# Fused conditioned attention on one core: the opening's load queues, one transposed chunk and three score bursts' banks are rearranged

## The chip, the core and the metric

The kernel runs on one core of a Trainium2 chip. The core has five engines that run side by side and meet through semaphores: TensorE (PE) multiplies matrices into PSUM, VectorE (DVE), ScalarE (ACT) and GpSimd (POOL) work elementwise, and SyncE (SP) issues transfers. PSUM has eight banks of 128 x 512 f32. Transfers can be issued from SP's queue or from ACT's; an engine takes its instructions in the order in which they stand, so whatever waits at the head of a queue holds up all that is behind it.

The metric is the device time of one execution in microseconds (us). The three timed runs of the kernel before took 762.27, 764.2 and 765.88 us; the median, 764.2 us, is its time.

## The reference

x has 8 batches of 512 rows and 512 columns (f32). There are 16 heads of 32 columns. `tokens` is the condition, one row for each batch.

```python
Q = _split_heads(x @ Wq.T + bq)
K = _split_heads(x @ Wk.T + bk)
V = _split_heads(x @ Wv.T + bv)
tQ = _split_heads(tokens @ Wq.T + bq)
tK = _split_heads(tokens @ Wk.T + bk)
cQ = Q + tQ
cK = K + tK
scores = einsum('bhqd,bhkd->bhqk', cQ, cK) / sqrt(HEAD_DIM)
attn = softmax(scores, axis=-1)
out = einsum('bhqk,bhkd->bhqd', attn, V)
return x + out
```

## The kernel before

The work is cut into 32 steps `t` (8 batches by 4 groups `g` of 128 columns, four heads in each). For a step, four chunks `qc` of 128 query rows are treated one after the other: a **burst** of four score matmuls (`row_scores`, L433, one head each, each shown as two passes in the profile, so x8) fills four banks, DVE takes the row maxima of two banks at a time (`row_max_of`, L442), and ACT makes the exponentials of these banks only to add up the denominators (`denominators`, L470, tile `dead`). Later the scores are made again transposed, with the maxima subtracted by a small matmul (L512, L515), ACT makes the exponentials `e` (L527, L529), and PE multiplies them with v (L534). The maxima reach the matmul as bf16 parts that POOL makes (`split_max`, L484 to L487) and PE transposes (`transpose_max`, L496). Projections are made in part by a fast scheme with seven products of half blocks (`first_products`, `other_products`, products at L335 and L338), which need sums of blocks of the weights (`combine_w`, POOL) and of x (`combine_x`).

The order of all work on PE, ACT, DVE and POOL is the order in which it is written (a manual schedule); the order of transfers is that of each issuing queue. A load needs a semaphore; there are eight for them in turn, so a later load waits, on its queue, for the landing of the load that holds its semaphore.

Everything before the loop `for t in range(T - 3)` is the **opening**. It loads four chunks of x (x0 to x3) and 12 chunks of weights (256 KB each), transposes them on PE (`transpose_x` L251, evacuated at L254; `transpose_w` L206, evacuated at L213 to L219), projects q and k of step 0 directly (L281), brings in the condition, and then runs the four bursts of step 0 and the first of step 1 between further projections.

Which bank is used where is written out by hand: `psum` is one tile of eight banks, `TURNS` holds one row for each burst, `banks(i)` is the i-th number in the current row, and `advance()` goes to the next. The places 4 to 7 of a row are the burst's four banks, in two pairs. The opening's bursts use rows 13 to 17:

```python
(2, 5, 0, 1, 6, 7, 3, 4),     # row 13: row_max(0, 0)
(2, 5, 3, 4, 6, 7, 0, 1),     # row 14: row_max(0, 1)
(0, 1, 5, 2, 6, 7, 3, 4),     # row 15: row_max(0, 2)
(0, 1, 5, 2, 6, 7, 3, 4),     # row 16: row_max(0, 3)
(5, 0, 6, 7, 1, 2, 3, 4),     # row 17: row_max(1, 0)
```

So the burst of `row_max(1, 0)` writes banks 1, 2, 3, 4, right after the burst of `row_max(0, 3)` in 6, 7, 3, 4. With `other_products("v", 0, 0, ..., (2, 0))` the products of v go to banks 6 and 5, and the maxima are transposed into bank 7.

The loads of the opening stand in this order. SP: x0, x2, the condition, bq, bk, Wq chunk 0, Wq 2 and 3, Wk 1 to 3, Wv 0 to 3, bv, then x4 to x7. ACT: x1, x3, Wk 0, Wq 1, and behind them the load of its table of functions with a first exponential (L193).

Of the kernel before, what the change touches and what calls it, by code (L numbers as in the profile page):

```python
# [17 lines left out]
def kernel(  # L18
# [33 lines left out]
    nc = tc.nc  # L52
    P = 128
    B, S, D = x.shape
# [5 lines left out]
    NS = S // P  # L60
# [33 lines left out]
        (2, 5, 0, 1, 6, 7, 3, 4),  # L94
        (2, 5, 3, 4, 6, 7, 0, 1),
        (0, 1, 5, 2, 6, 7, 3, 4),
        (0, 1, 5, 2, 6, 7, 3, 4),
        (5, 0, 6, 7, 1, 2, 3, 4),
    ]
    turn = [0]  # L100
# [1 line left out]
    def banks(i, n=1):  # L102

        j = TURNS[turn[0]][i]
        return psum[:, j, :] if n == 1 else psum[:, j : j + n, :]
# [13 lines left out]
    def load_x(n, queue=nc.sync):  # L119

        if n < B * NS:
            xs[n] = xp.tile([P, D], F32, tag="x", name=f"x_{n}")
            queue.dma_start(xs[n], x[n // NS, n % NS * P : (n % NS + 1) * P, :])
# [17 lines left out]
    def load_w(n, w, queue, cs=range(NC)):  # L141
        wv = w.rearrange("(c p) d -> p c d", p=P)
        for c in cs:
            queue.dma_start(ws[n][:, c, :], wv[:, c, :])
# [16 lines left out]
    load_x(3, nc.scalar)  # L161

    cond_sb = const.tile([B + 2, D], F32, tag="cond", name="cond_sb")
    nc.sync.dma_start(cond_sb[:B, :], cond)
    nc.sync.dma_start(cond_sb[B : B + 1, :], bq.rearrange("(o d) -> o d", o=1))
    nc.sync.dma_start(cond_sb[B + 1 : B + 2, :], bk.rearrange("(o d) -> o d", o=1))
    load_w("q", Wq, nc.sync, [0])
    load_w("k", Wk, nc.scalar, [0])
    load_w("q", Wq, nc.scalar, [1])
    load_w("q", Wq, nc.sync, [2, 3])  # L170
    load_w("k", Wk, nc.sync, [1, 2, 3])
    load_w("v", Wv, nc.sync)
    bvb = const.tile([P, D], F32, tag="bvb", name="bvb")
# [28 lines left out]
    def transpose_w(n, dc, pt, odd=None):  # L202

        odd = dc % 2 if odd is None else odd
        for cc in range(NC):
            nc.tensor.transpose(  # L206
                pt[:, cc * P : (cc + 1) * P], ws[n][:, dc, cc * P : (cc + 1) * P], ident
            )
        o = wT[n][:, :, dc * P : (dc + 1) * P]
        pv = pt.rearrange("p (c s) -> p c s", c=NC)  # L210
        if n == "q":
            if odd:
                nc.vector.tensor_scalar(o, pv, SCALE, None, ALU.mult)  # L213
            else:
                nc.scalar.activation(o, pv, AF.Copy, scale=SCALE)
        elif odd:
            nc.vector.tensor_copy(o, pv)
        else:
            nc.scalar.copy(o, pv)  # L219
# [3 lines left out]
    def combine_w(n):  # L223


        wc[n] = stage.tile([P, 4, 2, HS], F32, tag="w", name=f"wc_{n}")
        if n == "v":
            blk = wT[n].rearrange("p k (two f) -> p k two f", two=2)
            blk = [[blk[:, j * 2 : j * 2 + 2, i, :] for j in range(2)] for i in range(2)]
            to = [wc[n][:, i, :, :] for i in range(4)]  # L230
        else:
            blk = wT[n].rearrange("p k (u two f) -> p k u two f", u=2, two=2)
            blk = [[blk[:, j * 2 : j * 2 + 2, :, i, :] for j in range(2)] for i in range(2)]
            to = [wc[n][:, i, :, :].rearrange("p k (u f) -> p k u f", u=2) for i in range(4)]
        nc.gpsimd.tensor_tensor(to[0], blk[1][0], blk[1][1], ALU.add)
        nc.gpsimd.tensor_tensor(to[1], to[0], blk[0][0], ALU.subtract)
        nc.gpsimd.tensor_tensor(to[2], blk[0][0], blk[1][0], ALU.subtract)
        nc.gpsimd.tensor_tensor(to[3], blk[0][1], to[1], ALU.subtract)
# [4 lines left out]
    def transpose_x(n, pt, leaves=nc.vector.tensor_copy):  # L243

        b, sc = divmod(n, NS)
        if b >= B:
            return
        if sc == 0:
            xT[b] = xtp.tile([P, NC, S], F32, tag="xT", name=f"xT_{b}")
        for cc in range(NC):  # L250
            nc.tensor.transpose(  # L251
                pt[:, cc * P : (cc + 1) * P], xs[n][:, cc * P : (cc + 1) * P], ident
            )
        leaves(xT[b][:, :, sc * P : (sc + 1) * P], pt.rearrange("p (c s) -> p c s", c=NC))  # L254
        load_x(n + NS)
# [17 lines left out]
    def pair_of(t, n):  # L273

        if (n, t // 2) not in pairs:
            pairs[n, t // 2] = qkp.tile([P, 2, S], F32, tag=n, name=f"{n}T_{t // 2}")
        return pairs[n, t // 2]
# [50 lines left out]
    def product(n, b, u, i, pt, kcs=(0, 1), cols=None):  # L328


        for kc in kcs:
            w = block_of_w(n, i, u, kc)
            if n == "v":
                xb = block_of_x(b, i, kc, slice(u * P, (u + 1) * P))
                nc.tensor.matmul(pt, xb, w, start=(kc == kcs[0]), stop=(kc == kcs[-1]))  # L335
            else:
                xb = block_of_x(b, i, kc, cols or slice(0, HS))
                nc.tensor.matmul(pt, w, xb, start=(kc == kcs[0]), stop=(kc == kcs[-1]))  # L338

    def twice(a):  # L340
        return a.unsqueeze(1).broadcast_to([P, 2, HS])

    def halves(a):
        return a.rearrange("p (h s) -> p h s", h=2)


    def parts_of(n, b, u):

        if n == "v":
            v = vs[b % 2]  # L350
            return v[:, u::2, :HS], v[:, u + 2, :HS], v[:, u::2, HS:], v[:, u + 2, HS:]
        o = pair_of(b * G + u * 2, n)
        return halves(o[:, 0, :]), o[:, 0, HS:], halves(o[:, 1, :]), o[:, 1, HS:]

    def plus(n, b, u, g, o, pt, rest):

        if n == "v":
            nc.vector.tensor_tensor(o, pt, rest, ALU.add)
        else:
            add = tok[:, "qk".index(n), u * 2 + g, b : b + 1]  # L360
            nc.vector.scalar_tensor_tensor(o, pt, add, rest, ALU.add, ALU.add)
# [22 lines left out]
    def other_products(n, b, u, dens, small, at):  # L384

        dens()
        one_, two_ = banks(at[0]), banks(at[1])
        product(n, b, u, 4, one_[:, :HS])
        product(n, b, u, 5, one_[:, HS:])
        small()  # L390
        if n == "k":
            product(n, b, u, 2, two_[:, :P], (1,), slice(0, P))
            product(n, b, u, 2, two_[:, P:HS], (1, 0), slice(P, HS))
        else:
            product(n, b, u, 2, two_[:, :HS], (1,))
        product(n, b, u, 3, two_[:, HS:])
        c1, c12, c2, c22 = parts_of(n, b, u)
        nc.vector.tensor_tensor(c12, one_[:, HS:], c12, ALU.add)
        nc.vector.tensor_tensor(c2, halves(one_), twice(c22), ALU.add)
        plus(n, b, u, 0, c1, halves(two_), c1)  # L400
        if n != "v":
            for g in range(2):
                qkT[n, b * G + u * 2 + g] = pair_of(b * G + u * 2, n)[:, g, :]
# [60 lines left out]
    def denominators(t, qc, prs=range(NP)):  # L464

        if t >= T - 1:
            return
        for j in [pr * 2 + i for pr in prs for i in range(2)]:
            dead = op.tile([P, S], F32, tag="dead", name=f"dead_{t}_{qc}_{j}")
            nc.scalar.activation(  # L470
                dead,
                banks(HG + j),
                AF.Exp,
                bias=nmax[t][:, qc, j, :],
                accum_out=sums[t][:, qc, j, :],
            )
# [14 lines left out]
    def transpose_max(t, bank, copy=nc.vector.tensor_copy):  # L491
        if t >= T:
            return
        pt = bank.bitcast(BF16)
        for qc in range(NS):
            nc.tensor.transpose(  # L496
                pt[:, qc * P : (qc + 1) * P],
                split[t % 2][:, qc, :, :].rearrange("p h e -> p (h e)"),
                identb,
            )  # L500
        maxT[t] = op.tile([P, S], BF16, tag="maxT", name=f"maxT_{t}")
        copy(maxT[t], pt[:, :S])
# [125 lines left out]
    def bank(i):  # L628
        return psum[:, i, :]
# [37 lines left out]
    project_qk_end(0, "k", pk)  # L667
    transpose_w("v", 3, bank(4), 1)
    transpose_x(NS, bank(2), nc.scalar.copy)
    for n in ("q", "k", "v"):  # L670
        combine_w(n)

# [3 lines left out]

    turn[0] = 13
    row_max(0, 0)
    transpose_x(NS + 1, banks(0), nc.scalar.copy)
    denominators(0, 0)  # L680
    project_qk(1, "q", banks(3))
    project_qk(1, "k", banks(1))
# [11 lines left out]
    first_products("v", 0, 0, lambda: denominators(0, 3), nothing, 2, 0)  # L694
    advance()
    row_max(1, 0)
    transpose_max(0, banks(3), nc.scalar.copy)
    other_products("v", 0, 0, lambda: denominators(1, 0), nothing, (2, 0))
    load_residual(0)
    turn[0] = 0  # L700

# [25 lines left out]
    for t in range(T - 3):  # L727
# [53 lines left out]
        def small():  # L781
            transpose_max(t + 1, banks(1))
            if t and r % 2 == 0:
                output(t - 1, banks(2))
# [145 lines left out]
```

## Time and profile before

| What | Value |
|---|---|
| median of three runs | 764.2 us |
| the profiled execution itself | 762.58 us |
| its span, first to last instruction | 760.8 us |
| granted TensorE clock, mean over the span | 0.999 |
| DMA, mean over the span | 39 GB/s |
| DMA in the opening, 5 to 20 us | 311 to 371 GB/s |
| opening, start to first loop instruction on PE | 55.45 us |

The page of the profile gives each engine's busy time, the chain of waits that ended last, and groups of equal instructions. A timeline row gives start, duration, engine, line, operation, output<-inputs, shapes and count; where the engine was idle before it, the idle time and what ended it stand in square brackets. `PE` rows are matmuls, `PEld` rows the weight loads that go with them, `SPq` and `ACTq` rows the issue of a transfer. PE's ends are modelled: where two groups follow each other without a bracket, the difference of their starts is the time that the first one held PE. A chain row for a transfer gives the time of issue and the time until it landed.

The edited places lie at 0.7 to 10 us (loads, table, first transposes), 24 to 27 us (x4, x5 and the first burst) and 45 to 57 us (the last burst of step 0, the first of step 1, the transposed maxima and the products of v).

### The profile page before, as it was taken

Reading aid. Unit: us, or ns where it says so; the run is one execution under the profiler, and the core shown is the slowest. Engines: PE = TensorE matmul, PEld = TensorE weight load, DVE = VectorE, ACT = ScalarE, POOL = GpSimd, SP = SyncE. Lnnn points to the kernel's source line nnn. Section 1 sums busy time; section 2 is a strip of 40 time slices with the busy share of each in tenths; the row PEclk is TensorE's granted clock in tenths of the full one; section 3 lists DMA queues with packets and bytes.
Section 4 is the critical chain, followed back from the end, with each engine's and each line's share of the span. In section 5 each row is a group of like instructions: output and inputs, shape, how many; then the busy total and the mean of one; then the engine's idle time right before and its main releaser. Section 6 shows DMA issues by size and latency. Waiting matters only on the chain.

```text
span 760.8 us, 14393 instructions
## 1 busy us (share of the span) xinstructions
PE 750.4 (99%) x5494; PEld 435.9 (57%) x5494; DVE 525.2 (69%) x730; ACT 630.2 (83%) x1462; POOL 132.9 (17%) x229
## 2 busy tenths in 40 slices
PE   8999999999999999999999999999999999999997
PEld 5566556655556665565665555665555665555432
DVE  2577767677667777676776776777766777757764
ACT  2559888888889888888888888888888988888965
POOL 2711011111101111101111111111110111110220
PEclk9999999999999999999999999999999999999999
DMA  9200011102011110111111011110101111000110
GB/s 310 64 2 15 15 43 43 43 15 56 15 42 43 43 31 13 47 39 43 42 32 40 15 43 42 43 44 14 43 1 28 29 28 28 1 29 29 29 42 28
DMA packets 40376, 29.51 MB, mean 39 GB/s; under 512 B 1770, under 2 KB 34538, under 8 KB 40308
## 3 DMA queue, kind: packets, MB, share of 16 engines
q1 hardware_dynamic: 39460, 27.42, 12.6%
q10 hardware_dynamic: 848, 1.18, 0.5%
q8 instruction: 43, 0.70, 0.4%
q14 instruction: 25, 0.20, 0.1%
HBM read 20.21 MB, written 8.39 MB: 38 GB/s over the span
## 4 chain that ended last, share of the span: by engine, by line
PE 96%; ACT 1%; DMA 1%; DVE 0%; issue 0%; DVEq 0%
PE psum L338 25%; PE psum L534 15%; PE psum L515 15%; PE psum L433 14%; PE psum L335 14%; PE psum L512 6%; PE psum L566 2%; PE psum L251 2%; PE psum L281 2%; PE psum L496 1%; ACT e L527 1%; DMA w_k<-in_L_cond_Wk_dram 1%; PE psum L206 1%; ACT e L529 0%; DMA x<-in_x_dram 0%
## 5 line engine op out<-in xcount | busy, mean ns | idle before, releaser
L442 DVE TENSOR_REDUCE nmax<-psum 128x2 f32<-128x1024 f32 x256 | 301.7, 1219 | 160.1 <-PE psum L433 159.4
L470 ACT ACTIVATE dead<-psum,nmax 128x512 f32<-128x512 f32 x496 | 335.0, 692 | 12.9 <-DVE nmax L442 12.8
L527 ACT ACTIVATE e<-psum 128x512 f32<-128x512 f32 x270 | 145.8, 595 | 81.5 <-PE psum L515 81.5
L433 PE MATMUL psum<-kT,qT 32*128 32x512 f32 x1024 | 138.1, 595 | 0.7 <-ACT kT L296 0.4
L515 PE MATMUL psum<-qT,kT 32*128 32x512 f32 x1024 | 132.5, 588 | 0.0
L529 ACT ACTIVATE e<-psum 128x1024 f32<-128x1024 f32 x121 | 124.7, 1030 | 0.0
L534 PE MATMUL psum<-e,v 128*32 128x512 f32 x1024 | 118.6, 596 | 0.4 <-ACT e L529 0.3
L470 ACT ACTIVATION_READ_ACCUMULATOR dead<-psum,nmax 128x1 f32 x496 | 103.6, 209 | 0.0
L484 POOL CAST split<-nmax 128x16 bf16<-128x16 f32 x32 | 8.2, 255 | 510.8 <-DVE nmax L442 510.8
L433 PEld LDWEIGHTS psum<-kT,qT 32*128 32x128 f32 x1024 | 63.8, 183 | 51.8 <-issue 29.4
L534 PEld LDWEIGHTS psum<-e,v 128*32 128x32 f32 x1024 | 29.5, 109 | 82.1 <-issue 57.9
L512 PE MATMUL psum<-maxT,onesb 3*128 3x512 bf16 x512 | 51.4, 384 | 1.6 <-DVE res L580 0.8
L515 PEld LDWEIGHTS psum<-qT,kT 32*128 32x128 f32 x1024 | 51.1, 185 | 2.5 <-issue 0.2
L591 POOL TENSOR_TENSOR res<-res,xr 128x512 f32<-128x512 f32 x30 | 38.1, 1271 | 66.1 <-DVE res L580 66.1
L335 PE MATMUL psum<-wc_v,xc 128*128 128x256 f32 x192 | 49.4, 380 | 0.0
L512 PEld LDWEIGHTS <-onesb 3*128 3x128 bf16 x512 | 13.4, 91 | 60.5 <-issue 50.9
L338 PE MATMUL psum<-xc,wc_q 128*128 128x256 f32 x180 | 46.4, 380 | 0.3 <-ACT e L529 0.3
L338 PE MATMUL psum<-xc,wc_k 128*128 128x256 f32 x180 | 46.3, 379 | 0.0
L556 DVE COPY oT<-psum 128x512 f32<-128x512 f32 x29 | 20.1, 691 | 35.6 <-PE psum L534 35.6
L135 POOL TENSOR_TENSOR xr<-xr,bvb 128x512 f32<-128x512 f32 x32 | 40.6, 1270 | 0.0
L335 PE MATMUL psum<-wT_v,xT 128*128 128x256 f32 x128 | 37.9, 398 | 0.0
L335 PEld LDWEIGHTS psum<-wc_v,xc 128*128 128x128 f32 x192 | 35.4, 190 | 4.3
(147 smaller groups left out, 831.0 us busy)
## 6 DMA issues: line engine op xcount, KB each, us to landing
xr<-in_x_dram SPq DMA_DIRECT2D x32, 256.0 KB, 3.1
out_dram<-res SPq DMA_DIRECT2D x31, 256.0 KB, 2.4
x<-in_x_dram SPq DMA_DIRECT2D x30, 256.0 KB, 2.7
w_v<-in_L_cond_Wv_dram SPq DMA_DIRECT2D x4, 256.0 KB, 5.5
w_q<-in_L_cond_Wq_dram SPq DMA_DIRECT2D x3, 256.0 KB, 4.4
w_k<-in_L_cond_Wk_dram SPq DMA_DIRECT2D x3, 256.0 KB
x<-in_x_dram ACTq DMA_DIRECT2D x2, 256.0 KB, 4.1
w_k<-in_L_cond_Wk_dram ACTq DMA_DIRECT2D x1, 256.0 KB, 4.5
```

The costliest lines, as they stand in the source:

```text
L135: nc.gpsimd.tensor_tensor(xr[t], xr[t], bias, ALU.add)
L335: nc.tensor.matmul(pt, xb, w, start=(kc == kcs[0]), stop=(kc == kcs[-1]))
L338: nc.tensor.matmul(pt, w, xb, start=(kc == kcs[0]), stop=(kc == kcs[-1]))
L433: nc.tensor.matmul(pt, qkT["q", t][r, qc * P : (qc + 1) * P], qkT["k", t][r, :], start=True, stop=True,)
L442: nc.vector.tensor_reduce(nmax[t][:, qc, pr * 2 : pr * 2 + 2, 0], pt, AX.X, ALU.max, negate=True)
L470: nc.scalar.activation(dead, banks(HG + j), AF.Exp, bias=nmax[t][:, qc, j, :], accum_out=sums[t][:, qc, j, :],)
L512: nc.tensor.matmul(bank[j], onesb[r, :], maxT[t][r, :], start=True, stop=False)
L515: nc.tensor.matmul(bank[j], qkT["k", t][r, kc * P : (kc + 1) * P], qkT["q", t][r, :], start=False, stop=True,)
L527: nc.scalar.activation(e[:, i, :], bank[pr * 2 + i], AF.Exp)
L529: nc.scalar.activation(e, banks(2, 2), AF.Exp)
L534: nc.tensor.matmul(pt[j * HD : (j + 1) * HD, :], vs[b % 2][:, kc, (g * HG + j) * HD : (g * HG + j + 1) * HD], es[t, kc, j // 2][:, j % 2, ...
L591: last.tensor_tensor(y, y, xr.pop(t), ALU.add)
```

## The change

- The three small loads into `cond_sb` (the condition, bq, bk) are issued by ACT instead of SP, behind x1 and x3. Wk 0 and Wq 1 are issued by SP instead of ACT, behind Wq 0. ACT's table load then stands behind x1, x3 and the three small loads.
- The transposes of x5 with their copy on ACT stand ahead of the first burst instead of behind it, and go to bank 5 instead of bank 2.
- Row 16 of `TURNS` has its two pairs in the other order, so that `row_max(0, 3)` fills banks 3, 4, 6, 7. The transposed maxima of step 0 go to bank 0 instead of 7, and the second half of the v products uses banks 5 and 6 in the other order.

```diff
-        (0, 1, 5, 2, 6, 7, 3, 4),
+        (0, 1, 5, 2, 3, 4, 6, 7),
...
-    nc.sync.dma_start(cond_sb[:B, :], cond)
-    nc.sync.dma_start(cond_sb[B : B + 1, :], bq.rearrange("(o d) -> o d", o=1))
-    nc.sync.dma_start(cond_sb[B + 1 : B + 2, :], bk.rearrange("(o d) -> o d", o=1))
+    nc.scalar.dma_start(cond_sb[:B, :], cond)
+    nc.scalar.dma_start(cond_sb[B : B + 1, :], bq.rearrange("(o d) -> o d", o=1))
+    nc.scalar.dma_start(cond_sb[B + 1 : B + 2, :], bk.rearrange("(o d) -> o d", o=1))
     load_w("q", Wq, nc.sync, [0])
-    load_w("k", Wk, nc.scalar, [0])
-    load_w("q", Wq, nc.scalar, [1])
-    load_w("q", Wq, nc.sync, [2, 3])
+    load_w("k", Wk, nc.sync, [0])
+    load_w("q", Wq, nc.sync, [1, 2, 3])
...
     transpose_x(NS, bank(2), nc.scalar.copy)
+    transpose_x(NS + 1, bank(5), nc.scalar.copy)
...
     row_max(0, 0)
-    transpose_x(NS + 1, banks(0), nc.scalar.copy)
     denominators(0, 0)
...
-    transpose_max(0, banks(3), nc.scalar.copy)
-    other_products("v", 0, 0, lambda: denominators(1, 0), nothing, (2, 0))
+    transpose_max(0, banks(1), nc.scalar.copy)
+    other_products("v", 0, 0, lambda: denominators(1, 0), nothing, (0, 2))
```

## The prediction

> **What bounds the kernel now.** I read the page's first line and busy row, then the chain of waits, then the timeline and the chain in order of time for the first 60 us, because every edit lies before the main loop.
>
> ```profile
> span 760.8 us, 14393 instructions
> PE 750.4 (99%) x5494; PEld 435.9 (57%) x5494; DVE 525.2 (69%) x730; ACT 630.2 (83%) x1462; POOL 132.9 (17%) x229
> PE 96%; ACT 1%; DMA 1%; DVE 0%; issue 0%; DVEq 0%
> ```
>
> TensorE (PE) sets the end: 99% busy, 96% of the chain. So only what moves PE counts, and the change can win only the time in which PE stands still or crawls in the opening. The timeline of PE from 0 to 57 us has three such places besides its start.
>
> ```profile
> 8.89 0.63 PE L206 MATMUL psum<-ident,w_k 128*128 128x128 f32 x4 [1.16 <-DMA w_k<-in_L_cond_Wk_dram]
> 25.32 1.14 PE L433 MATMUL psum<-kT,qT 32*128 32x512 f32 x8 [0.39 <-ACT kT L296]
> 26.39 0.66 PE L251 MATMUL psum<-ident,x 128*128 128x128 f32 x4
> 49.93 2.18 PE L433 MATMUL psum<-kT,qT 32*128 32x512 f32 x8
> 52.04 0.40 PE L496 MATMUL psum<-identb,split 128*128 128x128 bf16 x4
> ```
>
> Columns: start, duration, engine, line, what, count, and in brackets the idle time before it and who ended it. See three things: 1.16 us of waiting for the first chunk of Wk; 0.39 us for kT; and a burst of eight score matmuls that takes 2.18 us where the same burst takes 1.14 everywhere else. The burst is slow without an idle bracket because half of it is held back; the weight loads show by whom:
>
> ```profile
> 50.99 0.29 PEld L433 LDWEIGHTS psum<-kT,qT 32*128 32x128 f32 x2 [0.38 <-ACT dead L470]
> ```
>
> **Part 1, the queues.** Before, ScalarE (ACT) issues two chunks of x, waits until chunk 0 of x has landed, issues Wk chunk 0, waits for chunk 2, issues Wq chunk 1, and only then loads its table:
>
> ```profile
> 4.22 0.34 ACTq L144 DMA_DIRECT2D w_k<-in_L_cond_Wk_dram  x1
> 5.52 0.34 ACTq L144 DMA_DIRECT2D w_q<-in_L_cond_Wq_dram  x1
> 5.88 1.28 ACT L193 ACT_TABLE_LOAD   x1 [5.88 <-DMA x<-in_x_dram]
> 7.29 1.05 ACT L254 COPY xT<-psum 128x512 f32<-128x512 f32 x2
> ```
>
> Wk0, issued at 4.22, lands 4.54 us later, at 8.76 (chain in order of time). Afterwards the three small loads (16 KB, 2 KB, 2 KB; 0.37, 0.23, 0.25 us of issue) leave SP and come behind x on ACT, and SP issues Wq0 at about 1.66, Wk0 at about 2.1, then Wq1 to Wq3. The built program has waits on SP at Wq1 (x0 landed, 4.20), Wq2 (x2, 5.50) and Wq3 (x3, 5.69), none at Wk0. The four x chunks still go first and share the same engines, so x stays at 4.20 to 5.69 and its transposes still end near 6.74. The weights then follow in the order of need: before, the chunks on SP alone land 0.67 us apart (12.58, 13.25, 13.93, 14.61 in the landing records). From Wq0 near 6.2 (6.34 before) this puts Wk0 near 6.9 and Wq1 near 7.6.
>
> PE then runs without the gap: bias and cond transposes 6.74, Wq0 7.08 (both as before), Wk0 at 7.53, Wq1 at 7.98 (a transposed chunk every 0.45 to 0.47, as from 9.56 to 10.03). The q projection needs wT_q0, which VectorE (DVE) has at 8.46 as before, so it starts at 8.49 instead of 10.03: **1.54 us won**. It also needs ACT's two copies of xT. ACT's last small load, bk, waits for x1 (4.38), so the table loads at about 4.7, not at 2.6; its first copy starts at 6.1, the second waits for PE's transposes (6.80) and ends at 7.42. That is 1.07 us of cover for the table's move. GpSimd's (POOL's) combinations of x start 0.9 earlier and bind nobody.
>
> A rule of the Trainium skill speaks against this part: "DMA: Bandwidth & Descriptors", section "Issuing engines are not separate DMA queues", says loads issued from different engines share the same 16 DMA engines, so that a change of issuer saves only the issue time. By it Wk0 would land as late as before and the part would be worth nothing on PE. The row says that Wk0 was late because its issue stood at 4.22 behind a wait and its packets then mixed with Wq2's, issued at 4.40; issue time and place in line do change. I take the row: 1.54 and not 0.
>
> The unknown is bk, now issued at about 4.40. PE's cond transposes wait for it, and every matmul is queued behind them; it costs nothing if landed by 6.61. Nearest row: Wk0, on ACT's queue at 4.22, had its first of 16 shares landed at 6.80, 2.58 later, of which some 0.6 are the seven further packets of 85 ns in a share; that leaves 1.98, so 6.38. Upper end by the undiminished 2.58: 6.98, which costs 0.37. Worst row: Wk0's full 4.54, so 8.94, a cost of 2.33. I take 6.38 and zero; less is impossible, since the x transposes end at 6.74 anyway.
>
> **Part 2, the chunk of x.** PE's 0.39 gap at 25.32 is the wait for kT, which ACT ends at 25.27. Four transposes now stand in it: they issue from 24.77 to 25.21, before kT is there, so the burst stays at 25.32 and the projection follows at 26.39 instead of 26.89: **0.50 us won**. Bank 5, their target, was emptied by DVE's qT (22.08 + 0.75 = 22.83) and is next written by the k projection, 3.4 us after the q projection starts; ACT's copy (0.59, behind x4's, so done by 26.35) is long over. On ACT it lies ahead of the exponentials, which wait for the maxima until 27.79: hidden. Its reload of x moves up on SP, from 27.08 to about 25.4 behind the 24.96 one; their order stays. If ACT were late with kT the gain would drop to 0.39.
>
> **Part 3, the banks.** Today's burst at 49.93 has its last two heads in banks 3 and 4, which the third and fourth exponential of the group before (49.48 and 50.15, read-out ended 50.27 and 50.94) still occupy. With that group's pairs swapped, 3 and 4 hold the first and second (read-out ended 48.93 and 49.60), free before 49.93. So the burst takes 1.07 from start to next start, as at 25.32, instead of 2.11: **1.04 us won**. What is late next, all on before's clock: the transposes of the maxima, now at 51.00, need POOL's split (semaphore 50.47) and the reader of bank 0 (DVE, 50.47): 0.5 to spare. Bank 6 is free at 50.27, bank 7 at 50.95; needed past 52 and at 54.4. ACT copies maxT 1.04 earlier, so the next four exponentials start with their maxima (52.33, 53.47) and release bank 4 near 55.1; DVE's last step on v ends near 55.3. The burst now at 56.54 wants both at 55.50: 0.2 to spare, the same as today (56.35 against 56.54). If one misses, the cost is the miss, up to the whole 1.04.
>
> **Sum:** 1.54 + 0.50 + 1.04 = 3.08 us, all of it time in which PE stands. From 55 us on PE has no gap over 0.03 us until 623 us, and nothing in the opening sits at a fixed time after the first loads, so the shift reaches the end. The profiled execution took 762.58 us (span 760.8): 759.5 (span 757.7). It lies 1.6 under the median of the runs, 764.2; from that median, **761.1**.
>
> **Rivals.** (a) One term fails, bk by 0.37 or more, or the stall returns at the next burst: 1.5 to 2.6 won, 762.2. For it: margins of 0.2; against: each margin also holds in before. (b) The loads are hidden in any order, as the rule says, and ACT or DVE takes back the rest before the loop: no change, 764.2. Against it: from 10.03 to 24.93 us ACT is busy for 3.90 and DVE for 5.29 us only, so neither can hold PE. (c) Slower: bk, alone on ACT's queue, is served only when SP's ring runs dry, after the last weight (landed 15.26 before). Cond would start near 15.2, the projection near 16.9, 6.9 late; less 1.54 from parts 2 and 3 this is 5.3 slower, 769.5. It decides from a landing past 6.61 + 3.08 = 9.69 on. For it: one packet against a queue of twelve chunks; against: Wk0 on ACT's queue and Wq2 on SP's advanced side by side (first shares at 6.80 and 7.47, last at 8.76 and 8.95).
>
> **Numbers.** Forecast 0.68, (a) 0.20, (b) 0.07, (c) 0.05. A measurement of this kernel tells about 0.5% (3.8 us) from no change; the three runs span 0.47%. The faster line is 760.4, between the two readings of the forecast (759.5 and 761.1), so half of its 0.68, and a fifth of (a), count as faster: 0.39. Slower is (c) and scatter in (b): 0.06; the rest, 0.55, within. Low: 759.5 less 1.6 of scatter, 757.9; high: 764.2 - 1.5 + 1.6 = 764.3.
>
> **What will show it.** The q projection starting near 8.5 with no wait for w_k; bk's landing read from PE's start of the cond transposes (6.74, or late); the burst at L433 following four transposes of x and then the projection 1.07 later; the slow burst at 1.1 and no 0.38 wait on ACT; span 757.7. A cond start past 7.1, a first w_k wait that survives, or a burst at L433 of more than 1.3 near 47 to 54 us would prove the step wrong.

## The result and the profile after

The changed kernel takes 760.91 us (median of 7 runs, 760.58 to 761.10) against 764.03 us for the kernel before (7 runs, 762.27 to 765.88, beside it on the same chip). The ratio is 0.9957, with a 95% interval of 0.9944 to 0.9971: 2.2 to 4.3 us less. The forecast was 761.1. But the forecast's other reading, the profiled execution, is missed: 759.5 us with a span of 757.7 was foreseen, 761.03 with a span of 759.2 came. So the median fits and the opening doesn't, and that is what the experiments are about.

The page after, its first line and busy row:

```profile
span 759.2 us, 14394 instructions
PE 749.0 (99%) x5494; PEld 435.0 (57%) x5494; DVE 525.2 (69%) x730; ACT 629.6 (83%) x1462; POOL 132.7 (17%) x229
```

PE is still the bound. First four rows of the kernel before, from which the differences below are taken: the first and the second q projection, the k projection behind the second, and the first instruction of the loop.

```profile
10.03 3.60 PE L281 MATMUL psum<-xT,wT_q 128*128 128x512 f32 x8
26.89 3.60 PE L281 MATMUL psum<-xT,wT_q 128*128 128x512 f32 x8
30.32 3.60 PE L281 MATMUL psum<-xT,wT_k 128*128 128x512 f32 x8
55.45 0.40 PE L512 MATMUL psum<-maxT,onesb 3*128 3x512 bf16 x4
```

The timeline of the changed kernel's opening (start, duration, engine, line, what, count, idle before and who ended it; lines past the loads are one lower than before):

```profile
4.39 2.29 PE L250 MATMUL psum<-ident,x 128*128 128x128 f32 x16 [0.17 <-DMA x<-in_x_dram]
7.92 0.41 PE L635 MATMUL psum<-ident,cond_sb 10*128 10x10 f32 x4 [1.24 <-DMA cond_sb<-in_L_cond_bk_dram]
8.26 0.66 PE L205 MATMUL psum<-ident,w_q 128*128 128x128 f32 x4
8.75 0.60 PE L205 MATMUL psum<-ident,w_k 128*128 128x128 f32 x4
9.19 0.60 PE L205 MATMUL psum<-ident,w_q 128*128 128x128 f32 x4
9.79 3.67 PE L280 MATMUL psum<-xT,wT_q 128*128 128x512 f32 x8
...
24.17 1.04 PE L250 MATMUL psum<-ident,x 128*128 128x128 f32 x8
25.17 1.14 PE L432 MATMUL psum<-kT,qT 32*128 32x512 f32 x8
26.24 3.70 PE L280 MATMUL psum<-xT,wT_q 128*128 128x512 f32 x8
...
49.38 1.14 PE L432 MATMUL psum<-kT,qT 32*128 32x512 f32 x8
50.45 0.40 PE L495 MATMUL psum<-identb,split 128*128 128x128 bf16 x4
...
53.86 0.39 PE L511 MATMUL psum<-maxT,onesb 3*128 3x512 bf16 x4
...
54.95 1.02 PE L432 MATMUL psum<-kT,qT 32*128 32x512 f32 x8
```

Four things are to be seen. The wait for Wk is gone and a new one of 1.24 us stands in front of the transposes of the condition: the bias bk. The 0.39 in front of the burst at 25 us is gone; x's transposes stand there, eight in a row. The burst at 49.38 takes 1.07 to the next start instead of 2.11. And the first loop instruction on PE (L511) starts at 53.86 instead of 55.45: 1.59 us earlier, the whole difference of the two spans; from it to the end it is 705.35 us here and 705.36 before.

The new wait in the chain in order of time (start, length, what):

```profile
0.73 3.78 DMA x<-in_x_dram
...
4.53 3.35 DMA cond_sb<-in_L_cond_bk_dram
```

and ACT's timeline around it:

```profile
4.53 0.23 ACTq L166 DMA_DIRECT2D cond_sb<-in_L_cond_bk_dram  x1
4.79 1.28 ACT L192 ACT_TABLE_LOAD   x1 [4.79 <-DMA x<-in_x_dram]
...
6.19 1.11 ACT L253 COPY xT<-psum 128x512 f32<-128x512 f32 x2
```

A load of 2 KB waits on ACT for x1 to land, is issued at 4.53 and is there 3.35 us later, at 7.87. The table and the copies behind it do what was foreseen; bk does not.

### The profile page after: what moved, and what is told of

Its sections match the earlier page's. It is cut to its first block, busy times and chain, and to the rows that moved or that the text cites. A ratio compares the mean times of both kernels' runs of the same rounds, so it can differ in the third digit from the quotient of the medians.

```text
span 759.2 us, 14394 instructions
## 1 busy us (share of the span) xinstructions
PE 749.0 (99%) x5494; PEld 435.0 (57%) x5494; DVE 525.2 (69%) x730; ACT 629.6 (83%) x1462; POOL 132.7 (17%) x229
## 4 chain that ended last, share of the span: by engine, by line
PE 96%; ACT 1%; DMA 1%; DVE 0%; issue 0%; DVEq 0%
PE psum L337 25%; PE psum L533 15%; PE psum L514 15%; PE psum L432 14%; PE psum L334 14%; PE psum L511 6%; PE psum L565 2%; PE psum L250 2%; PE psum L280 2%; PE psum L495 1%; ACT e L526 1%; PE psum L205 1%; DMA x<-in_x_dram 0%; ACT e L528 0%; DMA cond_sb<-in_L_cond_bk_dram 0%
## 5 line engine op out<-in xcount | busy, mean ns | idle before, releaser
L511 PE MATMUL psum<-maxT,onesb 3*128 3x512 bf16 x512 | 51.4, 384 | 1.6 <-DVE res L579 0.8
L511 PEld LDWEIGHTS <-onesb 3*128 3x128 bf16 x512 | 13.4, 91 | 60.5 <-issue 50.9
```

The lines of the kernel that those rows point to most:

```text
L511: nc.tensor.matmul(bank[j], onesb[r, :], maxT[t][r, :], start=True, stop=False)
```

## The experiments

Two questions: why the two medians are 3.1 us apart while the two profiles are only 1.6 apart, and which part of the change gives how much.

### The kernel before, again

The kernel before, timed and profiled three more times without an edit.

> The kernel before once more, with a profile. Its seven runs span 3.6 us (762.27 to 765.88), those of the change 0.5 us (760.58 to 761.10), and the profiled executions differ by 1.6 us where the medians differ by 3.1. Theory (loads): in the kernel before, Wk chunk 0 on ScalarE's queue and Wq chunk 2 on SyncE's share the DMA engines, and how they interleave differs from run to run; then PE's wait for w_k is not 1.16 us here, and the span is 759.6 plus that wait. Rival (loop): the wait for w_k is 1.16 within 0.1 and the span still differs from 760.8, by time lost after 56 us.

> A further look at the kernel before, to see where a longer run loses its time. Theory (loads): from the start of the first projection to the end it is 750.78 again, and the wait for w_k carries the whole difference in span: span = 750.78 + start of the first projection, which is 9.6 in the shortest look and would be 11 to 13 in a run of 764 to 766 us. Rival: the stretch after the first projection is longer.

> The same once more. Theory and rival as for the look before it.

Measured: 762.77 us (762.02 to 763.90, 10 runs; ratio to the other runs of the same kernel 0.9988, interval 0.9975 to 1.0001), and single times of 763.74 and 762.27. PE's timeline in the last two, the slower one first:

```profile
8.37 0.63 PE L206 MATMUL psum<-ident,w_k 128*128 128x128 f32 x4 [0.21 <-DMA w_k<-in_L_cond_Wk_dram]
10.68 0.63 PE L206 MATMUL psum<-ident,w_q 128*128 128x128 f32 x4 [1.68 <-DMA w_q<-in_L_cond_Wq_dram]
11.15 2.31 PE L281 MATMUL psum<-xT,wT_q 128*128 128x512 f32 x5
```

```profile
8.48 0.63 PE L206 MATMUL psum<-ident,w_k 128*128 128x128 f32 x4 [0.78 <-DVE wT_q L213]
9.24 0.63 PE L206 MATMUL psum<-ident,w_q 128*128 128x128 f32 x4
9.70 3.60 PE L281 MATMUL psum<-xT,wT_q 128*128 128x512 f32 x8
```

The first projection starts at 11.15 in the one and at 9.70 in the other, the spans are 761.9 and 760.5, and nothing else differs. The slower one's chain in order of time says what was late:

```profile
5.59 4.96 DMA w_q<-in_L_cond_Wq_dram
```

Wq chunk 1, the last load on ACT's queue, took 4.96 us there. In the four executions of this kernel it landed at 9.03, 9.11, 9.43 and 10.55, and the projection began 0.59 to 0.60 later each time: 9.63, 9.70, 10.03, 11.15. The expectations had named Wk chunk 0; the load that decides is Wq chunk 1. So the profile on which the prediction was made shows one of many openings, and none of its numbers for Wk and Wq is "the" number of the kernel.

### Part 1 alone, and two ways around bk

Only the queues of the change (the three lines of the small loads are drawn together into one in these cuts):

```diff
-    nc.sync.dma_start(cond_sb..., cond / bq / bk)
+    nc.scalar.dma_start(cond_sb..., cond / bq / bk)
     load_w("q", Wq, nc.sync, [0])
-    load_w("k", Wk, nc.scalar, [0])
-    load_w("q", Wq, nc.scalar, [1])
-    load_w("q", Wq, nc.sync, [2, 3])
+    load_w("k", Wk, nc.sync, [0])
+    load_w("q", Wq, nc.sync, [1, 2, 3])
```

> Only the load queues of the change. Theory (loads): the first projection starts 0.24 us earlier than before (9.79), held by bk; the span is 760.5 and the runs now agree within 0.8 us, median about 762.3, so 1.7 us under the kernel before, more than the two profiles show. Rival (loop): median about 763.8, and the runs spread over 3 us as before.

The whole change with the small loads back on SP:

```diff
-    nc.scalar.dma_start(cond_sb..., cond / bq / bk)
+    nc.sync.dma_start(cond_sb..., cond / bq / bk)
```

> The change with the three small loads back on SyncE, behind x2 and ahead of Wq chunk 0; all weights stay on SyncE. Theory (bk late): the cond transposes start at 6.8 us and not at 7.92, the first projection at about 8.6 and not at 9.79, the span is 758.0, 1.2 under the change. Rival (the weights themselves are not there before 9): PE waits for w_k or w_q instead, the first projection starts after 9.4 and the span is 758.8 or more.

The whole change with the transposes of cond (and the two bias results) moved behind the first projection, so that nothing on PE waits for bk ahead of it (cut, the moved lines shortened):

```diff
-    pc = bank(6)
-    ...
     for half in range(2):
         combine_x(0, half, nc.gpsimd)
     ...
         project_qk_part(0, "q", cc, pq)
+    pc = bank(6)
+    ...
```

> The change with the cond transposes (and the three VectorE steps behind them) moved behind the first projection of q; the loads are those of the change. Theory (bk late): nothing waits for bk any more; Wq chunk 0 is transposed at 6.7, the first projection starts at 8.5 when Wq chunk 1 (landed 7.91) is through, and the span is 757.9 to 758.0, 1.25 under the change, median about 759.7. Rival (the weights themselves are not there before 9): the first projection after 9.4, span 758.8 or more.

The columns "cond" and "first projection" give when the transposes of cond and the first q projection start on PE, in us.

| | median (range, runs) | ratio to before, interval | cond | first projection | span |
|---|---|---|---|---|---|
| queues only | 762.09 (761.76 to 762.57, 11) | 0.9982, 0.9973 to 0.9991 | 7.55 | 9.42 | 760.3 |
| small loads on SP | 760.79 (760.64 to 760.98, 5) | 0.9966, 0.9954 to 0.9979 | 6.66 | 9.47 | 758.8 |
| cond late | 760.48 (760.06 to 761.70, 5) | 0.9964, 0.9950 to 0.9978 | 12.45 | 8.85 | 758.8 |
| the change | 760.91 (760.58 to 761.10, 7) | 0.9957, 0.9944 to 0.9971 | 7.92 | 9.79 | 759.2 |

The queues alone are faster by the interval, and their eleven runs lie within 0.8 us where the kernel before beside them scatters over 3.9 (761.98 to 765.89, 21 runs). Seven of the 21 have a lowered clock (last section); the other fourteen lie between 761.98 and 763.54, with a median of 763.08, so against them the queues give 1.0 us. bk landed at 7.51 here (3.01 after its issue) and at 7.70 (3.05) with cond late: its lateness is no accident of one execution. What it costs differs: with the queues alone PE stood 0.44 for it and not 1.24, because the transposes of x ended later there.

With the small loads on SP, bk no longer holds anything, and another load does. PE's timeline of that kernel:

```profile
8.14 0.63 PE L205 MATMUL psum<-ident,w_k 128*128 128x128 f32 x4 [0.48 <-DMA w_k<-in_L_cond_Wk_dram]
9.01 0.63 PE L205 MATMUL psum<-ident,w_q 128*128 128x128 f32 x4 [0.24 <-DMA w_q<-in_L_cond_Wq_dram]
9.47 3.60 PE L280 MATMUL psum<-xT,wT_q 128*128 128x512 f32 x8
```

Now Wk0 is the ninth load. It takes x0's semaphore, waits for x0 (landed 4.42) and is issued at 4.44 instead of 2.11, so it lands at 8.00 instead of 7.28. In each of these kernels the first eight loads go out at once, and the ninth and the tenth wait for x0 and x1: Wk0 and Wq1 here, Wk0 and Wq2 in the kernel before, Wq1 (issued at 4.27) and bk (4.53) in the change. The expected 8.6 and 758.0 were missed; the rival was right.

With cond late the first projection comes 0.94 earlier than in the change, at 8.85. The moved transposes cost PE their time behind it, so the loop starts 0.46 earlier (53.40 against 53.86). The projection doesn't reach 8.5: in that execution the trace's first record of the full TensorE clock stands at 6.83 us (4.52 in the change's). The transposes of x ended later, then those of Wq chunk 0, and DVE's copy of these (8.01 to 8.70) set 8.85. The span of 757.9 to 758.0 and the median of 759.7 that were expected were not reached.

### bk from a queue where it doesn't wait

The whole change, with bk alone issued by GpSimd:

```diff
-    nc.scalar.dma_start(cond_sb[B + 1 : B + 2, :], bk.rearrange("(o d) -> o d", o=1))
+    nc.gpsimd.dma_start(cond_sb[B + 1 : B + 2, :], bk.rearrange("(o d) -> o d", o=1))
```

> The changed kernel with one edit: bk's 2 KB load is issued by GpSimd instead of ScalarE, where it waits for no earlier load (GpSimd's mask for the transposes comes right behind it) and neither ScalarE's queue nor SyncE's gets a wait in its place. My theory, that bk's landing (7.87 in the changed kernel, 7.51 and 7.70 in two others) is the term that the prediction mis-sized: bk lands before 6.7, the transposes of cond start near 6.75 and the first projection at 8.5 if the clock is released by 5.5, and by 8.9 at the latest (VectorE's copies held it at 8.83 to 8.85 in the two kernels where cond is late); 0.9 to 1.3 less than 9.79, so 759.6 to 760.2 in the median. Rival one: a 2 KB load that shares the 16 DMA engines with the weights lands about 3 us after its issue from any engine and is issued too late to help: cond near 7.9, 760.9. Rival two: GpSimd's issue holds up its mask, so that the transposes of x start later than 4.4 and everything behind them: 761 to 762.

PE's timeline:

```profile
6.67 0.41 PE L635 MATMUL psum<-ident,cond_sb 10*128 10x10 f32 x4
7.01 0.65 PE L205 MATMUL psum<-ident,w_q 128*128 128x128 f32 x4
7.50 0.60 PE L205 MATMUL psum<-ident,w_k 128*128 128x128 f32 x4
7.94 0.62 PE L205 MATMUL psum<-ident,w_q 128*128 128x128 f32 x4
8.54 3.67 PE L280 MATMUL psum<-xT,wT_q 128*128 128x512 f32 x8
```

This is the opening that the prediction worked out: 6.74, 7.08, 7.53, 7.98 and 8.49 stand there, 6.67, 7.01, 7.50, 7.94 and 8.54 here, without a bracket. The rival of the slow load was half right and lost all the same: bk took 4.7 us from GpSimd's issue at 1.24, longer than on ACT, but it was issued 3.3 us earlier and nothing waited for it. The loop starts at 52.61, 1.25 before the change's. The runs are less clear: 760.59 us (759.88 to 761.36, 6 runs), ratio 0.9948, interval 0.9930 to 0.9966, which overlaps with the change's. The 759.6 to 760.2 expected were missed. Two of the six have the lowered clock; the other four have a median of 760.40, 0.5 under the change's and not 1.25, so the profile's whole gain is not shown in the runs. The profiled execution lost 1.57 us again in its last 50 us, where the granted clock fell (last section), so its span is 759.5; with 705.36 from the loop on, as before and after, it would be 758.0.

### The projection ahead of Wq chunk 1

On top of cond late, the transposes of Wq chunk 1 are put behind the first projection, so that it needs neither bk nor Wq1 ahead of it on PE:

```diff
-    transpose_w("q", 1, bank(2), 1)
     pq, pk = bank(5), bank(0)
     for cc in range(NC):
         project_qk_part(0, "q", cc, pq)
+    transpose_w("q", 1, bank(2), 1)
```

> cond_late with the transposes of Wq chunk 1 moved behind the first projection, so that PE needs only Wq chunk 0 and Wk chunk 0 ahead of it. Theory: the first projection then starts when VectorE has evacuated Wq chunk 0, at 8.1 where the TensorE clock is released early and at 8.7 where late, 0.1 to 0.4 ahead of cond_late, median 760.1 to 760.4. Rival (what bounds is the evacuation plus the wait of the next chunk): no gain, 760.5.

Measured: 760.70 us (760.18 to 761.80, 10 runs), ratio 0.9967, interval 0.9956 to 0.9979: no gain over cond late. PE's timeline:

```profile
7.79 0.60 PE L205 MATMUL psum<-ident,w_k 128*128 128x128 f32 x4
8.83 3.67 PE L280 MATMUL psum<-xT,wT_q 128*128 128x512 f32 x8 [0.44 <-DVE wT_q L212]
```

The projection starts at 8.83, as with cond late (8.85): the transposes that went away only uncover a wait of 0.44 for DVE's wT_q, and are then paid for at 12.34. With the full clock late (again near 6.8 in this execution), the chain there is the transposes of x, those of Wq chunk 0 (7.35), and DVE's copy wT_q (7.99 to 8.69).

### Wq chunk 1 and the scatter

If Wq1's place on ACT's queue makes the scatter, moving it alone should take it away, and putting it back alone should bring it back. First the kernel before with Wq1 on SP, and nothing else:

```diff
     load_w("k", Wk, nc.scalar, [0])
-    load_w("q", Wq, nc.scalar, [1])
+    load_w("q", Wq, nc.sync, [1])
```

> The kernel before with one load moved: Wq chunk 1 from ScalarE's queue to SyncE's, behind Wq chunk 0; Wk chunk 0 stays on ScalarE. Theory (Wq chunk 1 second in line on ScalarE's queue is what varies: in four looks the first projection starts 0.59 to 0.60 us after it lands, at 9.03 to 10.55): the wide spread (762 to 765.9) goes, the runs agree within 1 us, median 762.0 to 762.5 with the first projection at 9.4 to 9.8. Rival (Wk chunk 0 is what varies): the spread stays over 2 us and PE waits for w_k in front of Wk chunk 0.

Then cond late (part 1 to 3 of the change in it) with Wq1 on ACT, behind the small loads:

```diff
-    load_w("q", Wq, nc.sync, [1, 2, 3])
+    load_w("q", Wq, nc.scalar, [1])
+    load_w("q", Wq, nc.sync, [2, 3])
```

> cond_late with Wq chunk 1 back on ScalarE's queue, behind bk. Theory: Wq chunk 1 is issued at 5.5 to 5.9 instead of 4.3 and lands at 9 to 11 instead of 7.97, PE waits 0.5 to 2.5 us for it, the first projection starts 0.6 after it lands; median 761.0 to 762.5 and runs over 1.5 us apart, where cond_late has 760.48. Rival (spread comes from elsewhere): median within 0.3 of cond_late and a spread as narrow as its.

The first: 762.46 us (762.11 to 764.69, 12 runs; ratio 0.9992, interval 0.9982 to 1.0001), ten of the twelve within 762.11 and 762.61. Wk0 landed at 8.23 and Wq1, issued at 4.35, at 8.42; the projection started at 9.27. Of these 0.76 us, 0.30 were lost again in the burst of part 3, which held PE for 2.42 there instead of 2.11, since the exponentials that it waits for came only 0.46 earlier. The second: 762.61 us (761.74 to 764.59, 12 runs; 0.9997, 0.9986 to 1.0007), 2.1 us more than cond late. Its scatter is no proof of the theory, because four of the twelve (763.81 and above) and one of the two high ones of the first kernel (763.84) have a mean clock of 0.997 (last section; the other high one, 764.69, has 0.998); the other eight lie between 761.74 and 762.67. PE's timeline of the second:

```profile
10.00 0.63 PE L206 MATMUL psum<-ident,w_q 128*128 128x128 f32 x4 [1.57 <-DMA w_q<-in_L_cond_Wq_dram]
10.47 2.74 PE L281 MATMUL psum<-xT,wT_q 128*128 128x512 f32 x6
```

Wq1 landed at 9.87 there, against 7.97 with cond late, and the projection followed 0.60 later: the place of one load is worth 1.62 us in these two profiles (10.47 against 8.85). Most of it is the time of issue, 5.82 against 4.31, since on ACT it stands behind the landing of a later chunk of x (x3 instead of x0); the rest is a longer trip, 4.05 against 3.66 us. That Wq1 in this place is what delays the projection is shown by the two kernels; that it makes all the scatter is not.

### Part 2 alone

```diff
     transpose_x(NS, bank(2), nc.scalar.copy)
+    transpose_x(NS + 1, bank(5), nc.scalar.copy)
...
     row_max(0, 0)
-    transpose_x(NS + 1, banks(0), nc.scalar.copy)
```

> Only the transposes of x5 ahead of the first burst (part 2). Theory: they stand in the 0.39 us wait for kT; from the first projection to the end 0.41 to 0.50 shorter than before (750.28 to 750.37, before 750.78), no gap at the first burst. The spread of the runs stays wide. Rival: no gain, because kT comes later by as much.

Measured: 763.42 us (761.79 to 764.77, 12 runs), ratio 0.9990, interval 0.9980 to 1.0000; its profile has Wq1 late and the clock low at the end (last section), so the part is read from its own stretch. PE's timeline:

```profile
24.11 1.04 PE L251 MATMUL psum<-ident,x 128*128 128x128 f32 x8
25.10 1.14 PE L433 MATMUL psum<-kT,qT 32*128 32x512 f32 x8
26.18 3.70 PE L281 MATMUL psum<-xT,wT_q 128*128 128x512 f32 x8
29.71 3.60 PE L281 MATMUL psum<-xT,wT_k 128*128 128x512 f32 x8
```

From the first projection (9.80) to this second one it is 16.38 us, and 16.86 before (10.03 to 26.89): 0.48 won. But from here to the next group it is 3.53, and 3.43 before (26.89 to 30.32). A projection right behind the burst holds PE 0.10 longer than one behind transposes (3.70 against 3.60 in its row), and 0.10 goes back. From the first projection to the loop it is 45.04 against 45.42: part 2 gives 0.38.

### Part 3 alone

```diff
-        (0, 1, 5, 2, 6, 7, 3, 4),
+        (0, 1, 5, 2, 3, 4, 6, 7),
...
-    transpose_max(0, banks(3), nc.scalar.copy)
-    other_products("v", 0, 0, lambda: denominators(1, 0), nothing, (2, 0))
+    transpose_max(0, banks(1), nc.scalar.copy)
+    other_products("v", 0, 0, lambda: denominators(1, 0), nothing, (0, 2))
```

> Only the bank edits (part 3); loads and the place of x5 are those of before. Theory: the burst after the last one of step 0 takes 1.07 us to the next start and not 2.11; from the start of the first projection to the end the span is 1.04 shorter than before (749.74 and not 750.78). The spread of the runs stays wide (over 2 us), since it comes from when Wk chunk 0 lands. Rival: the stall only moves on, the stretch from the first projection to the end shrinks by less than 0.5; or the spread goes with the banks.

Measured: 762.74 us (761.16 to 764.67, 12 runs), ratio 0.9989, interval 0.9977 to 1.0001; the scatter of Wq1 (landed 10.02 in its profile) is in it. PE's timeline:

```profile
50.52 1.14 PE L433 MATMUL psum<-kT,qT 32*128 32x512 f32 x8
51.59 0.40 PE L496 MATMUL psum<-identb,split 128*128 128x128 bf16 x4
...
55.00 0.39 PE L512 MATMUL psum<-maxT,onesb 3*128 3x512 bf16 x4
56.09 1.02 PE L433 MATMUL psum<-kT,qT 32*128 32x512 f32 x8
```

The burst takes 1.07 to the next start, and from the first projection (10.62) to the end it is 749.73 us instead of 750.78. Part 3 gives 1.04 to 1.05, and the burst behind it (56.09) has no new wait.

## Why the prediction came out as it did

| Step | Foreseen | Measured |
|---|---|---|
| Wq0, Wk0, Wq1 landed | 6.2, 6.9, 7.6 | 6.59, 7.28, 7.91 |
| ACT's table, end of its copies of xT | 4.7, 7.42 | 4.79, 7.30 |
| bk: issue, landing, cost on PE | 4.40, 6.38, 0 | 4.53, 7.87, 1.24 |
| first projection | 8.49 | 9.79 (8.54 with bk out of the way) |
| part 2 | 0.50 | 0.38 |
| part 3 | 1.04 | 1.04 |
| span | 757.7 | 759.2 |
| from the profiled execution | 759.5 | 761.03 |
| from the median | 761.1 | 760.91 |

**Part 1, the order of the loads: right.** The weights came in the order of need, each within 0.4 us of the time foreseen and early enough. Wk's wait went, the table's move was hidden as said. The rule of the Trainium skill that was weighed against it ("DMA: Bandwidth & Descriptors", "Issuing engines are not separate DMA queues") says that another issuer saves only the time of issue. Read as "worth nothing", as the prediction read it, it did not hold here: in the pair above Wq1's landing moves by 1.90 us, of which 1.51 are its issue, because what an issuer saves includes the landings that its queue waits for.

**Part 1, bk: the term that failed.** The prediction put bk's landing 1.98 us after its issue, taken from the first share of Wk0 less the further packets of a share. Measured were 3.35 in the change, 3.01 with the queues alone and 3.05 with cond late. The start was late too by 0.13, so bk missed its cover (6.61) by 1.26, close to the 1.24 that PE stood. The upper end given (2.58, landing 6.98) was too low as well; only the worst row, 4.54, covered it. The term was taken from the first share of a load of another shape, with a deduction for its further packets. A nearer row stood in the trace of the kernel before and was not used, that of bk itself: issued by SP at 2.34, landed at 6.05, 3.71 later (3.48 to 3.55 in the three other profiles of that kernel). With 3.71 the sum would have had a landing at 8.11 and a cost of 1.50. It was rival (a)'s mechanism: one term fails and the rest stands. That bk was the cause in the profiled opening is shown by its bracket and by the kernel with bk on GpSimd, which has the foreseen opening to within 0.07 us. That edit also lets ACT load its table 2.25 us earlier, but ACT's copies of xT were done by 7.30 in the change, before bk landed. One smaller term was off too: from the end of DVE's wT_q to the projection the sum has 0.03 (8.46 to 8.49), and that kernel took 0.14 (8.40 to 8.54).

**Rival (b)**, no change because ACT or DVE takes the rest back, is excluded by the interval and by the loop's start, 1.59 earlier. The rule it leans on speaks of the time of issue alone and says nothing of loads that are hidden in any order.

**Rival (c)** had bk land only after the last weight, near 15. At 7.87 it didn't; it came 3.35 after its issue, in the midst of SP's weights.

**Part 2: right in place, 0.12 too large.** The wait for kT is filled as said (0.48). What the sum left out is the 0.10 that the projection loses when its first matmul follows the burst instead of transposes.

**Part 3: right**, by the size and by the margins: the next burst (54.95) has no wait in front of it.

**The balance.** Between the two profiles: 0.24 from the first projection (10.03 to 9.79), 0.41 from there to the second (part 2, of which 0.07 is lost again because the first projection now waits on DVE's copy for its first matmul), and 0.94 from the second to the loop (part 3 less the 0.10). That is 1.59, the difference of the spans.

**Why 761.1 was met all the same: luck.** The sum overstated part 1 against the profiled opening by 1.30 (bk), and two things that it did not know made this up. First, the profiled opening was one of the kernel's shorter ones. In the runs of the kernel before without the lowered clock (last section) the median is 763.2, 0.6 over the profiled execution, and the wait that made the longest of the four profiled openings longer than that one, the wait for Wq1, is what part 1 takes away. The queues alone gave 1.0 us against such runs, with bk's cost still in it; 1.54 was foreseen. Second, the seven runs before that stand beside the change's have a median 0.8 over the 763.2. Their clock is not on record, but two of them (765.54 and 765.88) lie above every run of that kernel without the lowered clock, and none of the change's seven has it. So of the 3.1 us between the medians some 2.3 are the change and some 0.8 the mix of runs before: an estimate from three medians (763.2 less 760.91, and 764.03 less 763.2). That the profiled execution lay 1.6 under the median had been noted; that this gap was in part what the change would remove, and in part something else, had not.

One sum of the prediction is off by a little: half of 0.68 and a fifth of 0.20 are 0.38, not 0.39. Nothing hangs on it.

## What to carry to other kernels

Before a stall is priced from one profile, compare several executions: a wait for a load that shares its queue with other loads can differ by 1.5 us between runs (Wq1 here), and what an edit gives is then a distribution made narrower, not a constant. Where loads of an opening outnumber the ones that may be issued without waiting, the first that wait are the late ones, however small they are; count them over all queues, put something there that nobody needs soon, and price it from its issue to its landing in the same crowd, best from the row of the very load where there is one. Here a load of 2 KB took hardly less time than one of 256 KB beside it (3.35 against 3.64 us in the change, issued 0.26 apart).

## What the runs showed of the hardware

- A 2 KB load (bk) took 3.0 to 3.4 us from issue to landing on ACT's queue beside SP's weights, 3.5 to 4.1 on SP's queue in the kernels that have it there, and 4.7 from GpSimd's. The 256 KB chunks that the change issues up to 6 us took 3.3 to 5.2.
- The time at which TensorE got its full clock in the opening differed from run to run, with the same warm-up in front. The trace's first record of it stands between 4.44 and 6.97 us in the fourteen profiles. Until then a transpose of x started every 0.21 us, afterwards every 0.11. (The clock of the profile's tables reads 1.00 before it too, where there is no record yet.) Where it came at 6.83 the sixteen transposes of x held PE until 7.37, and until 6.67 or so where it came early. The Trainium skill ("TensorE: Matmul & The Clock Gate", "Part 1: The HAM clock gate") says that the window over which activity is counted runs freely, so that the ramp differs between runs of one kernel. These runs agree in that; their spread of 2.5 us is wider than the 0.5 us to either side that the page gives.
- The granted clock also falls near the end in some executions: to a half, for 3.41 us. The profile of the kernel with part 2 alone, in a table by stretch (stretch, its length, busy times of PE, PEld, DVE, ACT and POOL, clock, DMA share, GB/s):

```profile
716.75:720.16 3.41, 2.27 (x33) 1.54 (x33) 3.23 (x4) 3.17 (x8) 0.19 (x1) 1.00 0.02 5
720.16:723.58 3.42, 3.42 (x20) 1.12 (x12) 0.86 (x1) 2.32 (x7) 1.08 (x1) 0.50 0.38 105
723.58:727.00 3.42, 3.42 (x32) 1.05 (x29) 2.76 (x3) 2.44 (x7) 0.63 (x3) 1.00 0.16 48
```

PE was busy for only 2.27 of the 3.41 us ahead of the fall. From the loop to the end this kernel then takes 706.90 instead of 705.36 us; the kernel with Wq1 back on ACT (707.07) and the one with bk on GpSimd (706.93) show the fall too. That is 1.54 to 1.71 us more, at most the half of 3.41.

When it falls can be read from the fourteen profiles. In the three that show it, the fall begins 713.39 us, 209 times 3.4133, after the first record of the full clock, and 665.3 to 665.6 us after the loop's start. Counted on in steps of 3.4133 us from their own first records, the nearest steps of the other eleven lie at 664.90 or before and at 666.18 or after, seen from the loop's start. So in these profiles the fall comes where such a step lies at one thin stretch of PE's work, and the place of the steps goes with the time of the first full clock, which differs from run to run. What is counted in a step is not shown: the first repetition of the kernel before has a step at 666.18 with PE as little busy ahead of it, and no fall.

Of the 82 runs of the kernel before that were timed beside the experiments, 26 have a mean clock of 0.997 or less, with a median of 765.3; the other 56 have 763.2 and lie between 761.98 and 764.34, which is the scatter of the loads and little else. (The profile with bk on GpSimd has the fall and a mean of 0.998, so the line between them is not sharp.) None of the 7 runs of the change and none of the 11 with its queues alone has 0.997 or less, but nor have the 10 repeated runs of the kernel before. The three kernels that show the fall in their profiles have the change or a part of it in them, so nothing here says that the change prevents it; why it is missing in those 28 runs stays open. It bears on the median before: against the 763.2, the change's 760.91 is 2.3 us less, and 3.1 only against the median with such runs in it.
